# The head of a graph-and-expert kernel: order and engines of the first row tile's loads, statistics and projection

## The chip, the cores and the metric

The kernel runs on one core of a Trainium2 chip. The time is the device time of one execution in microseconds (us), given as the median over several executions. A core has five engines with queues of their own, which wait for each other by semaphores: TensorE (PE; its weight loads are listed as PEld), VectorE (DVE), ScalarE (ACT), GpSimd (POOL) and SyncE (SP), which here issues DMAs only. Sixteen DMA engines move the data of all queues. PE writes its results to PSUM, in banks of 512 float32 per partition; DVE and ACT move them to SBUF.

## The reference

One layer on x (625 rows, 1024 columns) and a graph of 20000 edges with sources `src`, targets `dst` and types 0 or 1. First a graph block, then a mixture of experts; each adds its output to x:

```python
edge_index = jnp.stack([src, dst])
x = x + gnn(layernorm(x), edge_index, edge_type_2, ...)
x = x + ffn(layernorm(x)[None], ...)[0]

def gnn(h, ...):
    n = t5_layer_norm(h, ln_weight)                  # weight * n / rms(n)
    out = n @ W_root + bias                          # 1024 -> 286
    for r in range(2):
        w = (edge_type == r)
        sums = segment_sum((n[src] @ W_rel[r]) * w[:, None], dst)
        out = out + sums / maximum(segment_sum(w, dst), 1)[:, None]
    return h + elu(out) @ wo_weight                  # 286 -> 1024
```

The edges come sorted by target. `ffn` has two shared experts and the best two of eight for each row, with hidden size 256.

## The kernel before, in words

The kernel doesn't gather rows for edges. It counts for each pair (source row, target row and type) how many edges there are, and multiplies that matrix CT by the projected rows. The 625 rows are five tiles of 125 (`TP`, `NT`). The change is in the head of `sparse_kernel`; all behind the counts is left as it is.

*Loads* (lines 520 to 552). Edge types, targets and sources come as 80 rows of 250 numbers, on SP's and ACT's queues. Then x's tile 0, W_root, x's other tiles and the two W_rel on SP's queue, in that order.

*Edge columns* (`edge_columns`, line 664). DVE makes two row arrays `rowf` (source; target key, L667 to L672). PE transposes them into one PSUM bank `p_edge` (L677). ACT copies the keys to float16 columns `cols` (L687), each value twice; DVE splits each source into tile number and place in the tile (L690 to L692), ACT copies the place (L693), and DVE writes a code of the tile number (L695).

*Statistics and h* (`stats`, line 753). For a row tile, DVE runs bn_stats on two halves of x (L757) and bn_aggr (L758), and makes the negative mean `neg` (L760); ACT subtracts the mean from all 1024 columns (`h`, L765). `scales` (line 771) makes the factors from the variance; they are needed only when a projection is moved out of PSUM.

*Columns of h* (`to_columns`, line 789). PE transposes h in eight blocks into two banks (L795); ACT moves the first four (L801) and DVE the other four (L798) to `nT`, scaled by the norm's weight `lT`, which comes from a small transpose (L738, L739).

*Projections* (`project`, line 886). 15 products of a row tile with W_root or one W_rel (L891), 16 matmuls in float32 each. Numbers 0 to 4 are W_root, 5 to 9 and 10 to 14 the two W_rel.

*Counts* (`count_windows`, line 828). The edges are 160 groups of 125 (`EC`). For 4 or 8 of them at a time, DVE makes one-hot matrices of sources (L849, times the code L850) and of keys (L852), and PE multiplies them, a few narrow matmuls for each group (L868), into PSUM. After each group c, `between(c)` issues what was put there by hand with `at(c, ...)` (lines 984 to 1021): statistics, columns, scales, projections, `add_h`, aggregates. Projection 0 stands after group 7, 1 after 15, and 5 to 11 after 46 to 148.

*The order.* A scheduler turns the program into one queue for each engine, mostly in the program's order, by its own estimate of when operands are ready. `tc.issue_after(ins)` puts what is issued in its block behind `ins` on the same engine. PE's `warm(n)` (line 970) issues n matmuls on constants into `scrap` (L972) which nothing reads: 24 ahead of the edge columns and 40 behind them. `ps_mm` and `ps_acc` (lines 494 to 498) are two sets of three PSUM banks.

Of the kernel before, what the change touches and what calls it, by code (L numbers as in the profile page):

```python
# [8 lines left out]
F32 = mybir.dt.float32  # L9
# [9 lines left out]
D = 1024  # L19
# [433 lines left out]
def sparse_kernel(  # L453
# [43 lines left out]
    def ps_mm(name):  # L497
        return psum[0].tile([128, 512], F32, tag="mm", name=name, bufs=3)
# [23 lines left out]
    for name, v, eng in (("ety", edge_type, nc.sync), ("dst", dst, nc.scalar), ("src", src, nc.sync)):  # L522
        ti = fbig.tile([EH, 2 * EP], I32, name=f"{name}_i")
        eng.dma_start(ti, v.rearrange("(c p) -> c p", p=2 * EP))
        rows_i[name] = ti
# [12 lines left out]
    def load_x(t, n):  # L538
        nc.sync.dma_start(xh[:, t : t + n, :], bass.AP(tensor=x.tensor, offset=x.offset + t * TP * D,
                                                       ap=[[D, 128], [TP * D, n], [1, D]]))  # L540

    def load_w(r, w):
        nc.sync.dma_start(wg[:, :, r, :], w.rearrange("(k p) f -> p k f", p=128))

    load_x(0, 1)
    load_w(R, W_root)
# [117 lines left out]
    def edge_columns():  # L664
# [7 lines left out]
        nc.vector.tensor_copy(rowf[:, 0], rows_i["src"])  # L672
        p = ps_mm("p_edge")
        pv = p[:EP, : 2 * EC].rearrange("p (a j c) -> p a j c", a=2, j=2)
        for a in (0, 1):
            for j in range(2):
                nc.tensor.transpose(pv[:, a, j, :], rowf[:, a, j * EP : (j + 1) * EP], ident[:EH, :EH])  # L677
        wide = [EP, EH, 2, 2]

        def column(v):  # L680
            return v.rearrange("p (c j) b -> p c j b", j=2)

        def pairs(v):
            return v.rearrange("p j c -> p c j")[:, :, :, None].to_broadcast(wide)

        with tc.issue_after(table.ins):
            nc.scalar.copy(column(cols[:, KW_]), pairs(pv[:, 1]))  # L687

        q = fbig.tile([EP, 3, 2, EH], F32, name="q")
        nc.vector.tensor_scalar(q[:, 0], pv[:, 0], -float(TP // 2), 1.0 / TP, op0=ALU.add, op1=ALU.mult)  # L690
        nc.vector.tensor_scalar(q[:, 1], q[:, 0], ROUND, -ROUND, op0=ALU.add, op1=ALU.add)
        nc.vector.scalar_tensor_tensor(q[:, 2], q[:, 1], -float(TP), pv[:, 0], op0=ALU.mult, op1=ALU.add)  # L692
        nc.scalar.copy(column(cols[:, SP_]), pairs(q[:, 2]))  # L693

        return nc.vector.tensor_scalar(column(cols[:, VV_].bitcast(I16)), pairs(q[:, 1]), 4096.0, 7168.0,  # L695
                                       op0=ALU.mult, op1=ALU.add)

# [55 lines left out]
    def stats(t):  # L753
        st = small.tile([TP, 2, 6], F32, tag="st", name=f"st_{t}")
        for s in range(2):
            with tc.issue_after((second[0] if t > 1 else evicted[1] if t else behind).ins):
                nc.vector.bn_stats(st[:, s, :], xh[:TP, t, s * 512 : (s + 1) * 512])  # L757
# [3 lines left out]
        h = rows.tile([TP, D], F32, tag="h", name=f"h_{t}")  # L761
        with ExitStack() as order:
            if t == 1:
                order.enter_context(tc.issue_after(evicted[0].ins))
            moved = nc.scalar.activation(h, xh[:TP, t, :], AF.Identity, bias=neg)  # L765
# [61 lines left out]

    def count_windows(between):
        accs = []
        c0 = 0  # L830
        for g in GROUPS:
            oh_s = oneh.tile([EP, MAXG, 128], F16, tag="oh_s", name=f"ohs_{c0}")
            oh_k = oneh.tile([EP, MAXG, KR], F16, tag="oh_k", name=f"ohk_{c0}")

            def both(what, n):
                return [EP, g, n // 2, 2], cols[:, what, c0 : c0 + g][:, :, None, :].to_broadcast([EP, g, n // 2, 2])

            def halves(v):
                return v.rearrange("p g (a b) -> p g a b", b=2)

            order = ExitStack()
            if c0 == 0:
                order.enter_context(tc.issue_after(ahead.ins))
            elif c0 == 8:
                order.enter_context(tc.issue_after(second[0].ins))
            row = iota[:EP].rearrange("p (a b) -> p a b", b=2)
            shape, key = both(SP_, 128)
            os = halves(oh_s[:, :g, :])
            nc.vector.tensor_tensor(os, row[:, None].to_broadcast(shape), key, op=ALU.is_equal)  # L849
            nc.vector.tensor_tensor(os, os, both(VV_, 128)[1], op=ALU.mult)  # L850
            shape, key = both(KW_, KR)
            nc.vector.tensor_tensor(halves(oh_k[:, :g, :]), row[:, None, :SPAN].to_broadcast(shape), key,  # L852
                                    op=ALU.is_equal)
            order.close()
# [120 lines left out]
    warm(24)  # L975
    behind = edge_columns()
    transpose_lnw()
    warm(40)
    ahead = stats(0)
# [7 lines left out]
    for t, (c0, c1) in enumerate(((0, 3), (4, 9), (13, 19), (16, 22), (20, 26))):  # L987
        if t:
            at(c0, stats, t)
        at(c1, to_columns, t, None, nT, True)  # L990
# [11 lines left out]
    at(6, scales, 0, 2)  # L1002
    at(18, scales, 2, 4)
    at(21, scales, 4, NT)
    for i, c in enumerate((7, 15, 21, 24, 28, 46, 64, 82, 100, 118, 134, 148)):
        at(c, project, i)
# [21 lines left out]

    count_windows(between)
# [493 lines left out]
```

## Time and profile before

| what | value |
|---|---|
| median of four runs | 305.6 us (304.04 to 306.76) |
| the profiled execution | 304.4 us, its span 302.2 us |
| mean granted TensorE clock | 0.998 |
| busiest engines | PE 291.3 us, PEld 195.3, DVE 168.3, ACT 107.5 |
| costliest group | L891, 240 matmuls, 62.6 us |
| HBM read and written | 42.76 and 18.81 MB |

The page counts an engine as busy while an instruction of it runs; matmuls are pipelined, so that a busy PE is not PE at its peak. The span starts with the first instruction that the profiler records, and all times of lines count from there. The page's rows of digits cut the span in 40 slices of 7.55 us and give the busy share in tenths. The chain of work is followed back from the last instruction, at each step to what released it. In a timeline row stand start, duration, engine, line, operation, output and inputs, and in brackets how long the engine had been idle and what ended that.

### The profile page before, as it was taken

To read this page: it belongs to the slowest core of one execution; us is meant where nothing else is said; L and a number is where in the kernel's file an instruction comes from. 1 tells how busy PE (TensorE), PEld (TensorE's weight loads), DVE (VectorE), ACT (ScalarE), POOL (GpSimd) and SP (SyncE) were. 2 spreads that over 40 slices of the span, in tenths; PEclk is the share of its full clock that TensorE was granted. 3 is DMA by queue.
4 is the path that set the end of the run, shared out by engine and by line. 5 is a ranking of instruction groups with operands and counts; after the bars stand their busy time and mean duration, and the time that the engine had idled before them with its cause. 6 is when DMAs were issued, how large, how long until landed. Compare 5 with 4: busy or idle time off the path is not lost.

```text
span 302.2 us, 4682 instructions
## 1 busy us (share of the span) xinstructions
PE 291.3 (96%) x1649; PEld 195.3 (65%) x1649; DVE 168.3 (56%) x465; ACT 107.5 (36%) x246; POOL 45.0 (15%) x98
## 2 busy tenths in 40 slices
PE   8899999999999799999999999999999999999992
PEld 6677777787889534476777887887843334444451
DVE  5899999998327568756983122222223212256911
ACT  2455117355334432155123354738269311000000
POOL 9500000000000024240131212210003222200000
PEclk9999999999999999999999999999999999999999
DMA  7999920000009999965999253340056555489352
GB/s 220 318 307 389 421 84 2 0 2 1 0 14 344 348 348 391 399 196 169 353 399 410 86 197 102 109 141 2 0 213 257 221 215 219 176 316 377 138 149 62
DMA packets 27407, 61.15 MB, mean 202 GB/s; under 512 B 2175, under 2 KB 16006, under 8 KB 27374
## 3 DMA queue, kind: packets, MB, share of 16 engines
q1 hardware_dynamic: 21806, 43.77, 40.9%
q0 software_dynamic: 5280, 16.69, 15.9%
q10 hardware_dynamic: 294, 0.35, 0.5%
q8 instruction: 15, 0.25, 0.3%
q14 instruction: 12, 0.10, 0.1%
HBM read 42.76 MB, written 18.81 MB: 204 GB/s over the span
## 4 chain that ended last, share of the span: by engine, by line
PE 93%; DVE 4%; ACT 1%; issue 0%; ACTq 0%
PE p_pr L891 20%; PE p_h L1359 13%; PE p_yj L1417 13%; PE p_o L1472 11%; PE p_sh L1137 10%; PE p_y L952 6%; PE p_agg L909 6%; PE p_x L1340 3%; PE p_t L795 3%; PE cnt L868 2%; PE p_y L956 2%; PE p_hT L1371 1%; PE scrap L972 1%; PE p_gate L1085 1%; PE p_o L1474 1%; DVE ln_4s L727 0%
## 5 line engine op out<-in xcount | busy, mean ns | idle before, releaser
L891 PE MATMUL p_pr<-wg,nT 128*125 128x286 f32 x240 | 62.6, 410 | 0.0
L891 PEld LDWEIGHTS p_pr<-wg,nT 128*125 128x125 f32 x240 | 43.2, 187 | 11.5 <-ACT nT L801 0.5
L1359 PE MATMUL p_h<-w1a,xsT 128*128 (+2 forms) x176 | 40.0, 380 | 0.0
L1417 PE MATMUL p_yj<-w2a,hjT 128*128 (+2 forms) x88 | 38.6, 594 | 0.0
L1472 PE MATMUL p_o<-sw,shT 128*125 128x512 f32 (+1 forms) x88 | 36.1, 553 | 0.0
L1137 PE MATMUL p_sh<-h2T,sw 128*128 128x313 f32 (+1 forms) x128 | 35.2, 428 | 0.0
L1359 PEld LDWEIGHTS p_h<-w1a,xsT 128*128 128x128 f32 (+2 forms) x176 | 28.7, 168 | 7.4 <-issue 0.5
L1137 PEld LDWEIGHTS p_sh<-h2T,sw 128*128 128x128 f32 x128 | 23.7, 189 | 8.6 <-issue 0.2
L1417 PEld LDWEIGHTS p_yj<-w2a,hjT 128*128 128x128 f32 (+2 forms) x88 | 14.4, 168 | 22.4 <-issue 22.4
L1472 PEld LDWEIGHTS p_o<-sw,shT 128*125 128x125 f32 x88 | 16.4, 187 | 16.9 <-issue 16.2
L1421 DVE COPY ys<-p_yj 128x512 f32<-128x512 f32 x15 | 10.4, 692 | 28.7 <-PE p_yj L1417 27.0
L1363 DVE COPY hj<-p_h 128x256 f32<-128x256 f32 x11 | 4.7, 425 | 30.8 <-PE p_h L1359 30.8
L909 PE MATMUL p_agg<-P,CT 125*125 125x287 bf16 x150 | 20.1, 287 | 1.6 <-DVE agg L915 1.6
L909 PEld LDWEIGHTS <-CT 125*125 125x125 bf16 x150 | 18.5, 136 | 2.5 <-issue 2.0
L966 POOL DMA_DIRECT2D x1d<-xh x10 | 5.3, 530 | 98.0 <-DVE xh L959 98.0
L1425 POOL DMA_INDIRECT yt<-ys,row x11 | 10.8, 981 | 50.5 <-DVE ys L1421 50.5
L952 PE MATMUL p_y<-wo_t,eT 128*125 128x512 f32 x40 | 18.1, 595 | 0.0
L1332 POOL DMA_INDIRECT xs<-h2d,tok x11 | 11.1, 1013 | 45.0 <-PE p_x L1340 30.9
L1374 ACT ACTIVATE hjT<-p_hT,vT 128x128 f32<-128x128 f32 (+2 forms) x34 | 8.7, 332 | 24.5 <-PE p_hT L1371 24.5
L1344 DVE COPY xsT<-p_x 128x512 f32<-128x512 f32 x11 | 7.6, 692 | 17.4 <-PE p_x L1340 13.8
L1448 DVE SCALAR_TENSOR_TENSOR x<-p_o,x 125x512 f32<-125x512 f32 (+1 forms) x11 | 6.9, 640 | 16.3 <-PE p_o L1474 16.3
L1359 PE MATMUL p_h<-w1m,xsT 128*64 128x256 f32 (+1 forms) x96 | 14.7, 381 | 0.0
(302 smaller groups left out, 424.4 us busy)
## 6 DMA issues: line engine op xcount, KB each, us to landing
w1a<-in_L_ffn_W_dram SPq DMA_DIRECT2D x8, 1024.0 KB, 10.5
w2a<-in_L_ffn_W_dram SPq DMA_DIRECT2D x8, 1024.0 KB, 5.0
yt<-zero SPq DMA_DIRECT2D x2, 2560.0 KB
g<-yt SPq DMA_DIRECT2D x10, 512.0 KB, 6.6
sw<-in_L_ffn_sW_dram SPq DMA_DIRECT2D x4, 1024.0 KB, 5.0
x<-x1d SPq DMA_DIRECT2D x5, 500.0 KB
wg<-in_L_gnn_W_rel_dram SPq DMA_DIRECT2D x2, 1144.0 KB, 19.8
x1d<-xh POOLq DMA_DIRECT2D x5, 448.0 KB, 6.7
```

Of the source, the lines that this page charges most:

```text
L795: nc.tensor.transpose(pv[:, k, :], row[:, at : at + 128], ident[:TP, :TP])
L891: nc.tensor.matmul(p[:TP, :F], nT[:, k, m * TP : (m + 1) * TP], wg[:, k, r, :], start=(k == 0), stop=(k == KD - 1))
L909: nc.tensor.matmul(p[:TP, : F + 1], CT[:, m, at : at + TP], P[:, m, r, i], start=(m == 0 and i == 0), stop=(m == NT - 1 and i == 2))
L952: nc.tensor.matmul(ps[s][:TP, :], eT[:, k, :], wo_t[:, k, s * 512 : (s + 1) * 512], start=(k == 0), stop=False)
L1137: nc.tensor.matmul(p[:, : z - a], sw1[:, i, k, t * 128 : (t + 1) * 128], h2T[:, k, a:z], start=(k == 0), stop=(k == KD - 1))
L1332: nc.gpsimd.indirect_dma_start(out=xs, out_offset=None, in_=h2d, in_offset=bass.IndirectOffsetOnAxis(ap=tok[:, j : j + 1], axis=0))
L1340: nc.tensor.transpose(p[:, k * 128 : (k + 1) * 128], xs[:, at : at + 128], ident)
L1359: nc.tensor.matmul(p[a:b, :H], xsT[j][:, k, a:b], w1m[j, a][:, 0, k, :] if a else w1a[:, bass.ds(e, 1), k, :], start=(k == 0), stop=(k == ...
L1417: made = nc.tensor.matmul(p[a:b], hjT[:, j, k, a:b], w2m[j, a, k][:, at] if a else w2a[:, bass.ds(e, 1), k, at], start=(k == 0), stop=(k = ...
L1421: nc.vector.tensor_copy(y[:, at], p)
L1425: sent.append(nc.gpsimd.indirect_dma_start(out=yt, out_offset=bass.IndirectOffsetOnAxis(ap=row[:, j : j + 1], axis=0), in_=y, in_offset=No ...
L1472: nc.tensor.matmul(p[:TP, :n], shT[:, i, k, own], sw2[:, i, k, at], start=(i == 0 and k == 0), stop=False)
```

## The change

- The three edge-row loads are all issued on ACT's queue. x's tile 0 becomes the first load on SP's queue, in two halves of 512 columns; W_root follows in two halves of its eight row blocks.
- `edge_columns` ends with the key copy. Its transposes go to two banks, sources to one of `ps_acc`, keys to one of `ps_mm`. The rest is a function of its own, `source_columns`, on DVE alone, which writes the places to `cols` directly; ACT's copy of them and one part of `q` are gone.
- Statistics of tile 0 are put behind the copy of the source rows (L672), ahead of the source columns.
- For tiles 0 and 1, ACT makes the first half of h and DVE the second. The others stay on ACT.
- The columns of tile 0 (`to_columns`) follow in the program ahead of all one-hots, and `one_hots`, taken out of `count_windows`, is called for the first group before that loop; then come statistics of tile 1, the scales of tiles 0 and 1 and projection 0, all ahead of the first count. The first one-hots are put behind the eviction of tile 0's columns, statistics 1 behind the second of these one-hot steps.
- `warm` issues 18 and 14 instead of 24 and 40.
- The hand-placed points move: columns 1 to 4 from 9, 19, 22, 26 to 3, 11, 14, 18; projections 1 to 4 from 15, 21, 24, 28 to 3, 12, 15, 20; 5 to 11 from 46 to 148 to 38 to 146.

```diff
-    for name, v, eng in (("ety", edge_type, nc.sync), ("dst", dst, nc.scalar), ("src", src, nc.sync)):
+    for name, v in (("ety", edge_type), ("dst", dst), ("src", src)):
...
-        eng.dma_start(ti, v.rearrange("(c p) -> c p", p=2 * EP))
+        nc.scalar.dma_start(ti, v.rearrange("(c p) -> c p", p=2 * EP))
...
-    load_x(0, 1)
-    load_w(R, W_root)
+    HALVES = [slice(s * 512, (s + 1) * 512) for s in range(2)]
+    for s in HALVES:
+        nc.sync.dma_start(xh[:, 0, s], x[:128, s])
+    load_w(R, W_root, slice(0, KD // 2), slice(KD // 2, KD))
...
-        nc.vector.tensor_copy(rowf[:, 0], rows_i["src"])
-        p = ps_mm("p_edge")
-        pv = p[:EP, : 2 * EC].rearrange("p (a j c) -> p a j c", a=2, j=2)
+        got = nc.vector.tensor_copy(rowf[:, 0], rows_i["src"])
+        ps = [ps_acc("p_edge"), ps_mm("p_edge_k")]
         for a in (0, 1):
             for j in range(2):
-                nc.tensor.transpose(pv[:, a, j, :], rowf[:, a, j * EP : (j + 1) * EP], ident[:EH, :EH])
...
+                nc.tensor.transpose(ps[a][:EP, j:EC:2], rowf[:, a, j * EP : (j + 1) * EP], ident[:EH, :EH])
 
         with tc.issue_after(table.ins):
-            nc.scalar.copy(column(cols[:, KW_]), pairs(pv[:, 1]))
-
-        q = fbig.tile([EP, 3, 2, EH], F32, name="q")
-        nc.vector.tensor_scalar(q[:, 0], pv[:, 0], -float(TP // 2), 1.0 / TP, op0=ALU.add, op1=ALU.mult)
+            nc.scalar.copy(cols[:, KW_], pairs(ps[1][:EP, :EC]))
+        return got, ps[0][:EP, :EC]
+
+    def pairs(v):
+        return v[:, :, None].to_broadcast([EP, EC, 2])
+
+    def source_columns(v, behind):
+
+        q = fbig.tile([EP, 2, EC], F32, name="q")
+        with tc.issue_after(behind.ins):
+            nc.vector.tensor_scalar(q[:, 0], v, -float(TP // 2), 1.0 / TP, op0=ALU.add, op1=ALU.mult)
         nc.vector.tensor_scalar(q[:, 1], q[:, 0], ROUND, -ROUND, op0=ALU.add, op1=ALU.add)
-        nc.vector.scalar_tensor_tensor(q[:, 2], q[:, 1], -float(TP), pv[:, 0], op0=ALU.mult, op1=ALU.add)
-        nc.scalar.copy(column(cols[:, SP_]), pairs(q[:, 2]))
-
-        return nc.vector.tensor_scalar(column(cols[:, VV_].bitcast(I16)), pairs(q[:, 1]), 4096.0, 7168.0,
+        nc.vector.scalar_tensor_tensor(cols[:, SP_], pairs(q[:, 1]), -float(TP), pairs(v),
                                        op0=ALU.mult, op1=ALU.add)
+
+        nc.vector.tensor_scalar(cols[:, VV_].bitcast(I16), pairs(q[:, 1]), 4096.0, 7168.0,
+                                op0=ALU.mult, op1=ALU.add)
...
-            with tc.issue_after((second[0] if t > 1 else evicted[1] if t else behind).ins):
+            with tc.issue_after((second[0] if t > 1 else first if t else behind).ins):
...
+        own, rest = (HALVES[0], HALVES[1]) if t < 2 else (slice(0, D), None)
...
-            moved = nc.scalar.activation(h, xh[:TP, t, :], AF.Identity, bias=neg)
+            moved = nc.scalar.activation(h[:, own], xh[:TP, t, own], AF.Identity, bias=neg)
+        if rest:
+            with tc.issue_after(last.ins):
+                last = nc.vector.tensor_scalar(h[:, rest], xh[:TP, t, rest], neg, None, op0=ALU.add)
...
+    def one_hots(c0, g):
...
+            if c0 < 8:
+                order.enter_context(tc.issue_after((second[0] if c0 else evicted[1]).ins))
+            nc.vector.tensor_tensor(os, row[:, None].to_broadcast(shape), key, op=ALU.is_equal)
+        last = nc.vector.tensor_tensor(os, os, both(VV_, 128)[1], op=ALU.mult)
...
+        return oh_s, oh_k, last
...
-    warm(24)
-    behind = edge_columns()
+    warm(18)
+    behind, sources = edge_columns()
     transpose_lnw()
-    warm(40)
-    ahead = stats(0)
+    warm(14)
+    source_columns(sources, stats(0))
+    to_columns(0, hs[0], nT, True)
...
-    for t, (c0, c1) in enumerate(((0, 3), (4, 9), (13, 19), (16, 22), (20, 26))):
+    for t, (c0, c1) in enumerate(((0, 3), (6, 11), (9, 14), (13, 18))):
         if t:
-            at(c0, stats, t)
-        at(c1, to_columns, t, None, nT, True)
+            at(c0, stats, t + 1)
+        at(c1, to_columns, t + 1, None, nT, True)
...
-    at(6, scales, 0, 2)
-    at(18, scales, 2, 4)
-    at(21, scales, 4, NT)
-    for i, c in enumerate((7, 15, 21, 24, 28, 46, 64, 82, 100, 118, 134, 148)):
-        at(c, project, i)
+    at(10, scales, 2, 4)
+    at(14, scales, 4, NT)
+    for i, c in enumerate((3, 12, 15, 20, 38, 56, 74, 92, 110, 128, 146)):
+        at(c, project, i + 1)
...
+    oh_s, oh_k, first = one_hots(0, GROUPS[0])
+    made[0] = oh_s, oh_k
+    stats(1)
+    scales(0, 2)
+    project(0)
     count_windows(between)
```

## The prediction

> **What bounds the kernel now.** I read the page first: busy shares, then the slices.
>
> ```profile
> span 302.2 us, 4682 instructions
> PE 291.3 (96%) x1649; PEld 195.3 (65%) x1649; DVE 168.3 (56%) x465; ACT 107.5 (36%) x246; POOL 45.0 (15%) x98
> PE   8899999999999799999999999999999999999992
> DVE  5899999998327568756983122222223212256911
> ```
>
> TensorE (PE) is busy 96% of the span, in nearly every slice of 7.55 us. So time can come only from PE doing something useless, or something useful at a poor time. DVE is full in the third to ninth slice (15 to 68 us): a second engine with no room there. Next, the chain of work that ended last, from the start:
>
> ```profile
> 2.53 2.67 PE scrap L972 x24
> 5.21 0.88 PE p_edge L677 x4
> ...
> 7.52 0.24 DVE cols L695
> 7.76 1.21 DVE st L757 x2
> ...
> 10.62 1.07 PE p_t L795 x8
> 11.70 0.11 PE cnt L868 x4
> 11.81 4.10 PE p_pr L891 x16
> ```
>
> From 10.62 us on the chain is PE, with two holes far behind (96.2 and 128.5 us), neither touched by the change. Before 10.62 PE does little but scrap, and the chain runs edge rows, edge columns, statistics of row tile 0, h, transposes. Here the change acts. The timeline shows the pieces:
>
> ```profile
> 4.06 0.29 DVE L672 CAST rowf<-src_i 80x250 f32<-80x250 int32 x1
> 6.57 0.32 DVE L690 TENSOR_SCALAR q<-p_edge 125x160 f32<-125x160 f32 x1 [2.21 <-ACT cols L687]
> 7.67 1.28 DVE L757 BATCH_NORM_STATS2 st<-xh 125x6 f32<-125x512 f32 x2
> 9.23 0.15 DVE L760 TENSOR_SCALAR neg<-mv 125x1 f32<-125x1 f32 x1
> 9.42 1.15 ACT L765 ACTIVATE h<-xh,neg 125x1024 f32<-125x1024 f32 x1 [1.40 <-DVE neg L760]
> 10.62 1.07 PE L795 MATMUL p_t<-ident,h 125*128 125x125 f32 x8
> 11.79 2.43 PE L891 MATMUL p_pr<-wg,nT 128*125 128x286 f32 x9
> ```
>
> DVE stands idle for 2.21 us behind the ACT copy out of the shared bank p_edge, then makes columns (6.57 to 7.76), then statistics. x of tile 0 is long there: in the trace's DMA packets its 128 packets of 4096 B run from 2.79 to 5.77 us. Last, the windows of half a microsecond, for PE's pace (second column in brackets: matmuls in the stretch):
>
> ```profile
> 6.50:7.00 0.50, 0.50 (x7) 0.50 (x6) 0.40 (x2) 0.10 (x2) 0.50 (x2) 1.00 1.08 384
> 7.50:8.00 0.50, 0.50 (x13) 0.50 (x11) 0.50 (x3) 0.44 (x1) 0.48 (x2) 1.00 1.99 341
> ```
>
> Equal scrap matmuls go at 0.111 us each at first (24 in 2.67 us) and at about 0.055 from 7.0 us on, though the granted clock reads 1.00 throughout.
>
> **The change part by part.** The sum is made on the profiled execution: 304.4 us, of which the span is 302.2. The four runs have a median of 305.6 (304.04 to 306.76), so that execution lies 1.2 under it; I take the gain off the median.
>
> *Loads.* The three edge-row loads all go on ACT's queue. The issues there take 0.43 (dst) and 0.58 us (lnw), so dst is issued at 1.2 instead of 0.74, src at 1.6 instead of 1.19, and ACT's table load moves from 1.81 to about 2.7, ending near 4.2; ACT's next work comes after p_edge, at 5.5 or later, which hides it. ety's use began at 3.16, 2.42 after issue, and src took 2.3 to land: dst would be there at 3.6, where L670 wants it (3.61), src at 3.9, under L672's 4.06. The halves of x are issued on SP at 0.74 and 1.2 instead of 1.65, so they now move beside the rows. The packets give the price: edge rows moved from 1.75 to 2.99; the first sixteen x packets took 0.72 to 1.34 us each, the others 0.159. Rows last behind all of x: some 1.3 us late; not at all disturbed: 0. I take 0.3, since most row packets (46 ns) are short and start before x's would be done. So the copy L672 ends between 4.35 and 5.6, taken 4.65, and x is whole at 4.4 to 5.0, about when its second half is asked for.
>
> *Statistics of tile 0.* From the first bn_stats to the end of neg: 9.38 - 7.67 = 1.71 us. Started at 4.65: neg at 6.4. Before, it was 9.38.
>
> *h in two halves.* ACT took 1.15 us for 1024 elements and 0.36 for 125 (L801), hence some 0.70 for 512: done at 7.1. DVE's half, by L731 (0.82 for 1024), 0.41: done at 6.85, beside ACT's. Key copy (0.42) and lT copy (0.17) precede on ACT, between about 5.8 and 6.5; they hold h up by 0.1 at most.
>
> *Scrap and edge transposes.* 18 instead of 24: 2.47 + 18 x 0.111 = 4.47, so p_edge starts when rowf is there, 4.6 to 5.0, instead of 4.90. p_edge to the next scrap took 1.3 us (4.90 to 6.20): the 14 start at 5.9 to 6.3. At 0.111 up to 7.0 and 0.055 behind, they end at 7.2 to 7.45; all at 0.111, at 7.45 to 7.85. So scrap and h are ready about together, and the transposes start at **7.3** instead of 10.62: **3.3 us**. Ends: 7.05 (rows undisturbed) and 8.3 (rows late).
>
> *Source columns.* One ACT cast (0.47) and one DVE operation go; a scalar_tensor_tensor with 320 outputs comes, 0.3 to 0.55 (L692, L901). All four (1.4 us) now lie between DVE's half of h (6.85) and the eviction of tile 0 (8.4): hidden by transposes. That the key's copy has its own bank ends the 2.21 us wait; late next is the copy L672, then neg.
>
> *First projection ahead of the counts.* From transposes to projection stays 1.17 us (10.62 to 11.79): it starts at 8.5. W_root's packets ran from 4.89 to 10.82, slowed from 7.3 on beside POOL's queue (4576 B packets of 0.64 us median); x leaves some 1.1 us earlier, so W_root should be in by about 7.5 to 9.7. Its second half is needed at 10.5: hidden; without that cover at most 0.3. The four counts that ran in a PE hole at 10.30 now cost: **-0.1**. Behind transposes 0 and 1 no counts fill the wait for the eviction any more: 0.1 each, **-0.2**.
>
> *PE's pace.* With 32 scrap matmuls less, pace could still be slow when transposes begin. In this record it rises at 7.0, so 0; if it rose only 4.5 us (2.47 to 7.0) after the transposes began, half of that, 2.2. I take **-0.1**, nearer the record, since PE stays busy without a break of note from 2.47 on.
> The Trainium skill, page "TensorE: Matmul & The Clock Gate", Part 1, speaks against fewer warm-up matmuls: the clock is halved until PE has been busy for a window of some 3.4 us, and that window runs free, so the moment varies between runs. The row agrees with a doubling, and shows one moment only. By the page alone (an estimate) the rise would fall anywhere from 5.9 to 9.3 us, and the mean loss would be 0.3 instead of 0.1, the time 0.2 longer.
>
> *x of tile 1.* Its packets end at 11.25 now, and statistics 1 start at 12.55. After: evict 0 ends on DVE at 9.2, two one-hot steps 0.7, so statistics 1 want it at 10.0; it should land 1.1 earlier, 10.15. DVE waits with everything queued behind; transposes 1 are wanted when the projection ends (12.7), h1 is ready at 10.15 + 1.71 + 0.7 = 12.55. Ends 0 and 0.8; taken **-0.1**.
>
> *Rows 2 to 4.* DVE must do, before transposes 2 at about 18.1: two evictions 1.3, three one-hot groups 2.6 (0.86 apiece, by starts 9.30 and 10.16), two statistics 3.4, half of h 0.4, scales 1.3: 9.0 from 9.0 on, plus h on ACT behind statistics 2, so 18.35. Ends 0 and 1.5; **-0.2**. The projections from the sixth on come 8 counts earlier, which gives PE work while DVE is behind; PE is no less full, cost 0 (cover: DVE keeping pace; see rivals).
>
> Sum: 3.3 - 0.1 - 0.2 - 0.1 - 0.1 - 0.2 = **2.6 us**. 304.4 - 2.6 = 301.8 for an execution like the profiled one; median 305.6 - 2.6 = **303.0**.
>
> **The rivals.**
> 1. *Everything fits* (transposes at 7.05, none of the four last losses but the counts): 3.55 - 0.1 = 3.4, 302.2. For: each loss is a near fit. Against: five near fits at once.
> 2. *Rows late behind x*: transposes at 8.3, gain 1.6, 304.0. For: the 1 us first packets of x. Against: rows are short packets on another queue.
> 3. *DVE gives it back at the end of the counts.* DVE gains only its 2.21 + 0.63 idle, less two halves of h (0.8) and the later rows (0.3): 1.7. The last counts start at 73.09, DVE's last one-hots end at 72.3, so PE may gain 1.7 + 0.8 = 2.5 before it waits there; if the last projections do not move ahead and DVE loses a further 1 to x of tile 1: 1.5, 304.1.
> 4. *Slower: DVE sets the pace of the first rounds.* Should one-hot groups of 8 (0.68 + 0.68 + 0.4 = 1.7 us) stand in DVE's queue ahead of statistics 2, 3 and 4, transposes wait. Slack before transposes 4 is 1.6 us (DVE's work 17.6 from 8.5, plus h 1.2, is 27.3; PE gets there at 28.9). It decides at 2.6 + 1.6 = 4.2 us of such work, 2.5 groups. One group for each of three rounds: 5.1 - 4.2, 306.5; two: 10.2 - 4.2, 311.6; middle 309. For: DVE is full from 15 to 68 us. Against: statistics are asked for three to nine counts ahead of their transposes.
>
> **How the numbers follow.** Forecast 0.48 (its own range 302.1 to 303.9: transposes at 7.05 without the small losses but the counts, to 7.85 with 0.4 more of them), rival 1 0.20, rival 2 0.12, rival 3 0.11, rival 4 0.09. About 1% (3.06 us; 302.54 and 308.66) is what a measurement tells from no change. Faster by over 1%: rival 1 and three tenths of the forecast (0.44 of its range's 1.8, and some scatter of medians), 0.20 + 0.14 = 0.34. Slower by over 1%: most of rival 4, 0.07. Within: 0.59. Range: 301.3 (rival 1 less 0.9 of scatter, a third of the 2.7 between the runs before) to 305.2 (rivals 2 and 3 with about as much); outside lie rival 4 and a tenth of the rest.
>
> **What would show it.** Right: p_t first at 7.0 to 7.6, p_pr at 8.2 to 8.8, no DVE idle behind the key's copy, neg at 6.1 to 6.7, scrap pace doubling before 7.5. Wrong: L672 ending after 5.2 (rows late); PE waiting on h or x before transposes 1 or 2 for over 0.8; matmuls of the first projection at half pace; DVE ending its one-hots later than 70.8, with PE waiting there.

## The result

| | before | after | ratio, 95% interval |
|---|---|---|---|
| median | 305.04 us (303.62 to 307.36, 78 runs) | 305.72 us (304.49 to 308.13, 52 runs) | 1.0028 [1.0018, 1.0037] |
| profiled execution, its span | 304.4, 302.2 | 306.45, 304.5 | |

No difference by the 1% bound, and a little slower: 0.7 us, against a forecast of 2.6 less. 305.72 lies 0.5 above the range. The profiled pair stands 2.1 apart, three times what the medians say, so a profile's times show where something was lost and not what it is worth; prices below are by medians, or by the ratio to before on the same chip where that is said.

The page of the kernel after, the same four lines as shown of before:

```profile
span 304.5 us, 4623 instructions
PE 291.6 (96%) x1617; PEld 194.5 (64%) x1617; DVE 169.1 (56%) x467; ACT 106.6 (35%) x245; POOL 45.0 (15%) x98
PE   4999999999999799999999999999999999999992
DVE  4799999999526758765884122212223212238920
```

PE's first slice falls from 8 to 4: scrap is gone, and a hole is there instead. DVE's full stretch now ends a slice later (the tenth digit is 9, it was 8, and the eleventh 5 instead of 3). DVE is busy 0.8 us longer in all.

The chain of waits of after, from the start, and the first piece behind the projections, which will serve as a milestone (60 aggregate matmuls; in before they start at 88.77):

```profile
1.67 5.12 DMA src_i<-in_src_dram
6.88 0.30 DVE rowf L675
7.31 0.68 PE p_edge L679 x2
...
8.61 1.60 PE scrap L983 x14
10.22 1.67 PE p_t L802 x8
11.88 5.06 PE p_pr L902 x16
17.06 0.91 PE p_t L802 x8
...
90.85 7.47 PE p_agg L920 x60
```

The chain begins with a DMA of 5.12 us, which was not in it before. Transposes 0 start 0.4 to 0.6 us earlier than before (10.22 here, 10.01 by the timeline; 10.62 before), transposes 1 some 1.1 later, and by the milestone the kernel is 2.1 behind. The timeline of after:

```profile
4.17 0.42 DVE L670 TENSOR_TENSOR rowf<-ety_i,low 80x250 f32<-80x250 int32 x1 [1.42 <-DMA ety_i<-in_edge_type_dram]
5.67 0.42 DVE L673 SCALAR_TENSOR_TENSOR rowf<-dst_i,rowf 80x250 f32<-80x250 int32 x1 [1.09 <-DMA dst_i<-in_dst_dram]
6.88 0.29 DVE L675 CAST rowf<-src_i 80x250 f32<-80x250 int32 x1 [0.79 <-DMA src_i<-in_src_dram]
8.64 0.15 DVE L762 TENSOR_SCALAR neg<-mv 125x1 f32<-125x1 f32 x1
8.83 0.73 ACT L769 ACTIVATE h<-xh,neg 125x512 f32<-125x512 f32 x1
8.83 0.49 DVE L772 TENSOR_SCALAR h<-xh,neg 125x512 f32<-125x512 f32 x1
10.01 1.87 PE L802 MATMUL p_t<-ident,h 125*128 125x125 f32 x8
11.68 5.27 PE L902 MATMUL p_pr<-wg,nT 128*125 128x286 f32 x16
```

Three brackets in a row say the same: DVE waits for an edge row three times, 3.3 us in all, and the source copy ends at 7.17 where the forecast had 4.65. From there to neg and to h all goes as long as forecast. Then two durations stand out: eight transposes in 1.87 us (1.07 before) and 16 matmuls in 5.27 (4.10). In the trace's DMA packets the 240 row packets, 1.75 to 2.99 us before, now run from 2.32 to 6.15, mixed in time with x's first tile (1.77 to 4.60) and W_root (from 3.97). SP's own waits show one thing more:

```profile
SPq L539 <- DMA ety_i<-in_edge_type_dram: 1.4, 1, 1.4
...
SPq L553 <- DMA dst_i<-in_dst_dram: 0.6, 1, 0.6
SPq L544 <- DMA src_i<-in_src_dram: 0.3, 1, 0.3
```

(Waiting line, what was waited for, us in total, times, longest.) SP, which only issues loads, now waits for the edge rows to land; x of tile 1 is issued at 4.08 instead of 2.59. In after statistics 1 lose nothing by it: they start at 13.57 without a wait for x.

### The profile page after: what moved, and what is told of

The parts are those of the page before. It is cut to its first block, busy times and chain, and to the rows that moved or that the text cites. A ratio compares the mean times of both kernels' runs of the same rounds, so it can differ in the third digit from the quotient of the medians.

```text
span 304.5 us, 4623 instructions
## 1 busy us (share of the span) xinstructions
PE 291.6 (96%) x1617; PEld 194.5 (64%) x1617; DVE 169.1 (56%) x467; ACT 106.6 (35%) x245; POOL 45.0 (15%) x98
## 4 chain that ended last, share of the span: by engine, by line
PE 89%; DVE 6%; DMA 2%; ACT 1%; issue 1%; ACTq 0%; DVEq 0%
PE p_pr L902 17%; PE p_h L1375 13%; PE p_yj L1433 13%; PE p_o L1488 11%; PE p_sh L1153 10%; PE p_y L963 6%; PE p_agg L920 6%; PE p_x L1356 3%; PE p_t L802 2%; PE p_y L967 2%; DMA src_i<-in_src_dram 2%; PE cnt L879 2%; DVE st L759 1%; PE p_hT L1387 1%; PE p_gate L1101 1%; PE p_o L1490 1%
## 5 line engine op out<-in xcount | busy, mean ns | idle before, releaser
L902 PE MATMUL p_pr<-wg,nT 128*125 128x286 f32 x240 | 64.7, 416 | 0.1
```

The costliest lines, as they stand in the source:

```text
L902: nc.tensor.matmul(p[:TP, :F], nT[:, k, m * TP : (m + 1) * TP], wg[:, k, r, :], start=(k == 0), stop=(k == KD - 1))
```

## The experiments

Two theories stood at first. A: the late rows take the gain. B: PE's half pace takes it. Two more came up early. C: DVE, full from some 15 us on, sets the pace of the rounds and when the counts end, so that an earlier start of PE is given back there. D: x of tiles 1 and 2 lands too late for an earlier start. A table first; times in us, the last three columns by each profile (the last one-hot of DVE ends; the last counts of PE start; the milestone).

| run | median | ratio to before | one-hots | counts | milestone |
|---|---|---|---|---|---|
| before | 305.04 | | 72.3 | 72.9 | 88.77 |
| after | 305.72 | 1.0028 [1.0018, 1.0037] | 75.5 | 75.6 | 90.85 |
| e1 rows first | 307.02 | 1.0060 [1.0033, 1.0086] | 76.6 | 76.7 | 91.94 |
| e2 rows on one queue | 307.53 | 1.0081 [1.0050, 1.0112] | 78.0 | 78.1 | 93.32 |
| e3 more scrap | 305.11 | 1.0002 [0.9979, 1.0026] | 74.2 | 74.2 | 89.50 |
| e4 loads alone, on before | 306.30 | 1.0046 [1.0025, 1.0066] | 74.4 | 75.0 | 90.82 |
| e5 e1, bias late | 305.05 | 1.0018 [0.9984, 1.0051] | 74.3 | 74.4 | 89.65 |
| e6 e5, more scrap | 305.78 | 1.0002 [0.9971, 1.0033] | 74.3 | 74.4 | 89.66 |
| e7 bias late, on before | 304.20 | 0.9966 [0.9945, 0.9986] | 72.2 | 72.8 | 88.66 |
| e8 e1, more scrap | 306.81 | 1.0047 [1.0021, 1.0074] | 76.1 | 76.2 | 91.46 |
| e9 after, add_h late | 304.04 | 0.9987 [0.9966, 1.0008] | 63.4 | 73.0 | 88.88 |
| e10 e6, x split | 303.61 | 0.9966 [0.9948, 0.9983] | 73.3 | 73.3 | 88.58 |
| e11 e6, points earlier | 304.17 | 0.9969 [0.9947, 0.9992] | 76.9 | 79.2 | 91.06 |
| e12 all together | 301.78 | 0.9920 [0.9891, 0.9949] | 63.6 | 74.8 | 86.71 |
| e13 before, add_h late | 305.11 | 1.0019 [1.0000, 1.0039] | 61.4 | 73.3 | 89.17 |
| e14 before, three helpers | 304.76 | 1.0001 [0.9989, 1.0014] | 60.6 | 72.5 | 88.37 |
| e15 after, h on ACT | 305.05 | 1.0012 [0.9992, 1.0031] | 75.0 | 75.0 | 90.31 |
| e16 after, three helpers | 304.03 | 0.9929 [0.9900, 0.9959] | 64.2 | 73.9 | 89.77 |
| e17 e12, rows late | 303.95 | 0.9940 [0.9906, 0.9973] | 66.1 | 77.3 | 89.17 |
| e18 e12, less scrap | 302.90 | 0.9884 [0.9846, 0.9922] | 65.3 | 76.5 | 88.39 |

The ratio is to before on the same chip. Before's median read 304.7 to 305.1 there, but 306.35 beside e16 to e18 (single runs from 303.4 to 307.3), so that these three ratios flatter: by medians against 304.8, e16 is 0.8 us under before and not 2.2. A profile is one execution; that of e11 (306.14) lies 2 us above its median.

**e1 and e2: the rows.** The rows' loads as in before, ahead of x on two queues; or all on SP, ahead of x.

```diff
-    for name, v in (("ety", edge_type), ("dst", dst), ("src", src)):
-        nc.scalar.dma_start(ti, ...)
+    for name, v, eng in (("ety", edge_type, nc.sync), ("dst", dst, nc.scalar), ("src", src, nc.sync)):
+        eng.dma_start(ti, ...)        # e2: nc.sync for all three
```

> The changed kernel with its edge-row loads put back as they were (types and sources on SP ahead of x, targets on ACT); the order on PE, DVE and ACT is the changed one. Theory A (the rows come 2.8 us late because x's halves and W_root share the DMA engines with them): the copy of the source rows ends at 4.4 to 4.8 instead of 7.16, first transposes at 7.4 to 8.0 instead of 10.0, first projection at full pace; time 302.5 to 304.2. Theory B (the scrap matmuls taken out leave PE at slow pace): the first projection still takes 4.6 us or more, time 304.6 or more. Theory C (DVE sets the pace of the first rounds): the transposes of tile 0 come early, those of tile 2 no earlier than 20.5 (before 20.96), time 304.2 to 305.2.

> The changed kernel with all three edge-row loads on SP's queue ahead of x, so that they are one queue's first three loads but x and W_root come behind them. Theory A: third issue at 1.65, landing 2.3 later, so the source copy ends by 4.5 as in the run with the rows put back, and the time is within 0.5 us of it. Rival (three loads one after the other on one queue are what is slow): the source copy ends at 5.5 or later and the time is within 0.7 us of the changed kernel's 305.7.

e1 lies far above what theory A gave, and by medians both are slower than after (by 1.3 and 1.8). The timeline of e1:

```profile
3.97 0.29 DVE L675 CAST rowf<-src_i 80x250 f32<-80x250 int32 x1
...
8.27 1.93 PE L802 MATMUL p_t<-ident,h 125*128 125x125 f32 x8 [0.96 <-ACT h L769]
9.99 4.98 PE L902 MATMUL p_pr<-wg,nT 128*125 128x286 f32 x16
13.75 1.29 DVE L759 BATCH_NORM_STATS2 st<-xh 125x6 f32<-125x512 f32 x2 [1.79 <-DMA xh<-in_x_dram]
...
16.28 1.08 PE L802 MATMUL p_t<-ident,h 125*128 125x125 f32 x8 [1.20 <-ACT h L769]
```

The rows are mended to the tenth (the copy ends at 4.26, in e2 at 4.08), and transposes 0 start 1.7 us earlier than in after. And yet nothing comes of it: statistics 1 start at 13.75 for want of x (13.57 in after), and transposes 1 at 16.28, still 0.5 behind before (15.80). In e2 statistics 1 wait 2.01, statistics 2 another 2.87. A alone falls as the cause of the time; the late rows are real, but x is next (D). e2 also shows that sharing one queue isn't what makes rows late, since its rows are the earliest: what delays them in after is x, whose packets start first. (Rows on ACT's queue with x held back were not run.)

**e3: the pace.** 24 more scrap matmuls ahead of the edge columns, in PE's hole.

```diff
-    warm(18)
+    warm(42)
```

> The changed kernel with 42 instead of 18 scrap matmuls ahead of the edge columns, which fill PE's 2.7 us hole while it waits for the rows; loads as changed. Theory A: h still comes at 9.6, only the pace is mended (first projection 4.1 instead of 5.1 us, transposes 0.9 instead of 1.7): 304.2 to 305.0. Theory B: the pace was all that was lost: 303.0 to 303.7. If DVE is the limit behind (theory C), nothing comes of it: 305.3 to 305.9.

```profile
9.51 1.07 PE L802 MATMUL p_t<-ident,h 125*128 125x125 f32 x8 [0.61 <-ACT h L769]
14.79 1.07 PE L802 MATMUL p_t<-ident,h 125*128 125x125 f32 x8
20.34 1.07 PE L802 MATMUL p_t<-ident,h 125*128 125x125 f32 x8
```

Pace is full here (1.07, and the projection 4.12): PE's scrap speeds up at 5.9 us. PE runs ahead of before by 1.1 us at transposes 0, 1.0 at transposes 1 and 0.6 at transposes 2 (20.96 in before). By the milestone it is 0.7 behind. B alone is worth 0.6 us by medians and 0.8 by ratios, and not the 1.7 that the profile lost; the rest goes between 20 and 75 us, where DVE is full.

**e4: the loads alone.** The kernel before with the loads of after, nothing else.

> The kernel before with the changed order of loads alone (rows on ACT, x's tile 0 and W_root in halves and first on SP). Theory A: the source copy ends at 7.0 to 7.3 instead of 4.35, and all behind it moves by 2.0 to 2.8 us: 307.0 to 307.9. Theory B: with all 64 scrap matmuls in place the time stays near that before, 305.0 to 305.6. Theory C: DVE is late by as much, so as theory A.

306.3: 1.3 us by medians (ratio 1.0046: 1.4), less than A gave and more than B. The source copy ends at 7.50, statistics 0 start at 9.89 instead of 7.67 and transposes 0 at 12.83 instead of 10.62, with PE at full pace. So the loads cost 2.2 us at that place, of which some three fifths show in the median.

**e5 to e8: x and the bias.** The convolution's bias goes to all 125 partitions in one load on POOL's queue. In e1's packets it moves from 7.4 to 11.2 us, 31 packets of 4576 B, 0.2 to 1.6 us each; beside it a few of W_root's packets take up to 0.45 us, where most take 0.05. e5 is e1 with this load on SP, behind x's last tile; e6 has 24 scrap matmuls instead of 14 as well, e7 is the kernel before with the bias late, e8 is e1 with the 24.

```diff
-    nc.gpsimd.dma_start(cb, bcast_rows(conv_bias, TP))
...
+    nc.sync.dma_start(cb, bcast_rows(conv_bias, TP))     # behind x, ahead of W_rel
...
-    warm(14)
+    warm(24)                                             # e6, e8
```

> The run with the rows put back, and the load of the bias cb taken off POOL's queue and put on SP's behind x's last tile. Theory D (with the rows in time the next limit is the landing of x's tiles 1 and 2 and of W_root's tail, held up by the 31 packets of 4576 B of the bias, 0.6 us each, at 7.4 to 11.2 us): statistics 1 start by 11.7 instead of 13.75, those of tile 2 do not wait for x at 17.75, transposes of tile 2 by 21.5 instead of 22.8; time 304.3 to 305.5 against 307.0, the first projection still at slow pace. Theory C (DVE's work, not x, sets the rounds): no change from 307.0 beyond 0.5.

> The same with 24 instead of 14 scrap matmuls behind the edge transposes, so that PE does not stand idle before tile 0's transposes. If landing and pace together are what ate the gain (D with B): first projection 4.1 us from about 9.4 on, transposes 1 by 14.2, transposes 2 by 20.3; time 302.7 to 304.0, faster than both kernels. If DVE sets the rounds (C): as the run without the added scrap, within 0.4.

> Control: the kernel before with the bias moved in the same way. It never waited for x's tiles 1 to 4 or W_root, so by theory D nothing comes of it: 304.7 to 305.4. A gain of over 0.5 would mean that the bias costs something beyond the head's loads.

> The run with the rows put back with 24 instead of 14 scrap matmuls behind the edge transposes, bias left on POOL's queue: pace alone. Theory D: x's tile 1 still lands at 13 to 14, so a faster first projection only waits longer: 306.2 to 307.2. Theory B (pace): 304.8 to 305.7.

e5 takes 2 us off e1: statistics 1 start at 11.60 without a wait, where e1 waited to 13.75. That is D, and it is the bias. But e5 is no faster than before. (Its statistics 2 still wait 1.28 us for x.) e6 has transposes 1 at 14.43 (before 15.80) and transposes 2 at 20.52 (20.96), and is no faster either, against a forecast of 302.7 to 304.0: its pace isn't mended (the projection takes 4.57), and DVE's last one-hots end at 74.3, 2.0 later than in before. e8, with the wait for x, gives nothing for its better pace: transposes 1 wait 1.33 us for h. e7 was to show nothing and gained 1.0 us by its ratio, with no transposes of its head moved by over 0.1; in e14, which has the same edit and two more, that gain isn't there. I take it for the size of error that such a ratio can have between builds; that `add_h` late hides it in e14 isn't excluded, since that edit alone reads 0.6 slower in before (e13).

**e9 and e13: DVE's load.** The five `add_h` (DVE adds h to x, for the layer's output) stand between the one-hots; they are moved behind the last count, in after and in before.

```diff
-    for t in range(NT):
-        at(40 + 16 * t, add_h, t)
...
+    for t in range(NT):
+        at(EC - 1, add_h, t)
```

> The changed kernel with its five add_h (DVE, 1.28 us each, between counts 40 and 104) moved behind the last count, where DVE has room; nothing else changed. Theory C (DVE, full from 20 us to its last one-hots at 75.5, is what PE's counts wait for): the last one-hots end near 70, the 0.5 us that PE falls back between 50 and 80 us comes back; the 1.7 lost before 30 us stay: 304.9 to 305.4 against 305.7. Rival (PE has work enough of its own there, DVE is only busy): no change, 305.5 to 305.9.

> The kernel before with one edit: the five add_h of each half, which DVE does between the one-hots, moved behind the last count. Theory C (in after DVE's one-hots set the end of the counts, in before they do not, since there the last one-hots end at 72.3 us and the last counts start at 73.09): 0 to 0.3 us, 304.7 to 305.1. Rival (the move is worth the same in any kernel of this kind, by what it takes off DVE and PE's semaphores, and the 1.7 us that it brought in after say nothing about after): 303.4 to 304.2.

The timelines at the end of the counts (DVE's last one-hot, PE's last counts), of before, after, e13 and e9:

```profile
71.65 0.68 DVE L850 TENSOR_TENSOR ohs<-ohs,cols 125x1024 f16<-125x1024 f16 x1
72.92 0.46 PE L868 MATMUL cnt<-ohk,ohs 125*128 125x58 f16 x11
```

```profile
75.13 0.39 DVE L857 TENSOR_TENSOR ohk<-iota,cols 125x464 f16<-125x464 f16 x1
75.58 0.37 PE L879 MATMUL cnt<-ohk,ohs 125*128 125x58 f16 x8
```

```profile
60.70 0.69 DVE L850 TENSOR_TENSOR ohs<-ohs,cols 125x1024 f16<-125x1024 f16 x1
73.32 0.46 PE L868 MATMUL cnt<-ohk,ohs 125*128 125x58 f16 x11
```

```profile
62.94 0.41 DVE L857 TENSOR_TENSOR ohk<-iota,cols 125x464 f16<-125x464 f16 x1
72.98 0.51 PE L879 MATMUL cnt<-ohk,ohs 125*128 125x58 f16 x13
```

In after the last counts start 0.06 us behind the end of the last one-hot, and 0.05 or 0.06 behind in e1, e2, e3, e5, e6, e8, e10 and e15 too, though their counts start anywhere from 73.3 to 78.1; in before 0.59 behind. The five `add_h` are 6.4 us of DVE (1.28 each); without them DVE's last one-hots come 11 us sooner in before and 12 in after, since some of the moves out of PSUM now also stand behind them. In before the counts come no sooner for it (73.32) and the time doesn't fall (305.11). In after the time falls by 1.7 us by medians, more than C gave, and by 1.2 by the two ratios, whose intervals don't overlap.

The counts of e9 come 2.6 earlier than those of after, but not all of that is the edit's. Transposes 1 of after and of e9, which stand ahead of every `add_h`:

```profile
16.90 1.05 PE L802 MATMUL p_t<-ident,h 125*128 125x125 f32 x8
```

```profile
15.67 1.08 PE L802 MATMUL p_t<-ident,h 125*128 125x125 f32 x8
```

1.2 us were there already, in a head that is the same program: e9's rows landed 0.4 earlier, and its PE reached full pace at 12.0 us instead of 14.1. From transposes 1 to the milestone after takes 73.95 us, e9 73.2 and e16 (below, it has the edit too) 73.0; before takes 73.0 and e13 73.4. So the edit is worth 0.7 to 0.9 us of that stretch and 1.2 to 1.7 of the time in after, and nothing in before: C holds, DVE's queue up to the last one-hot became a bound of that stage through the change. In before it is 0.6 us from being it. PE shows no hole for it; it is busy all the time from 70 to 80 us in after as well:

```profile
70.00:80.00 10.00, 10.00 (x63) 7.77 (x62) 8.25 (x17) 8.14 (x23) 0.00 (x0) 1.00 0.01 2
```

Matmuls of the projections behind (two at 74.27, two at 74.97) stand between the last counts there, so that no single wait shows the loss.

**e15: less on DVE, later transposes.** After, with h of tiles 0 and 1 whole on ACT.

```diff
-        own, rest = (HALVES[0], HALVES[1]) if t < 2 else (slice(0, D), None)
+        own, rest = slice(0, D), None
```

> The kernel after with h of row tiles 0 and 1 whole on ACT, so that DVE is relieved of two halves (0.49 us each) and transposes 0 wait some 0.45 us longer for h. Theory C (DVE's work up to the last one-hots sets the end of the counts): the last one-hots end 0.5 to 1 us earlier (75.5 in after) and the time falls by 0.3 to 0.8, to 304.9 to 305.4. Rival (the start of the transposes counts): 0.3 to 0.5 slower, 306.0 to 306.2.

305.05, ratio 1.0012 [0.9992, 1.0031] against 1.0028 of after: by medians 0.7 less, though transposes 0 start later (10.35); the last one-hots end 0.5 earlier (75.0), with the counts right behind. The intervals overlap, and the profile of e15 also has the faster projection (4.12 instead of 5.27), which the edit doesn't touch, so it leans to C and doesn't show it alone.

**e10 to e12: a version that uses the start.** e10 is e6 with x of tiles 2 and 3 in separate loads; e11 is e6 with the hand-placed points (scales too) earlier and projection 12 ahead of the last count; e12 has all of it and `add_h` late.

```diff
-    load_x(2, 2)
+    load_x(2, 1)
+    load_x(3, 1)                                                            # e10, e12
...
-    for t, (c0, c1) in enumerate(((0, 3), (6, 11), (9, 14), (13, 18))):
+    for t, (c0, c1) in enumerate(((0, 3), (3, 5), (5, 7), (7, 9))):           # e11, e12
...
-    for i, c in enumerate((3, 12, 15, 20, 38, 56, 74, 92, 110, 128, 146)):
+    for i, c in enumerate((3, 6, 8, 10, 28, 46, 64, 82, 100, 118, 136, 150)):
```

> The run with rows put back, bias late and more scrap, with x's tiles 2 and 3 in a load each instead of one of 1 MB. There statistics 2 waited for x until 15.49 and the transposes of tile 2 for h. Theory D (landing of x): statistics 2 start by 14.2, transposes 2 at 19.7 instead of 20.5, time 0.4 to 0.9 below that run (304.8 to 305.4). Theory C: DVE is behind by its own work, under 0.3 comes of it.

> The same run (rows put back, bias late, more scrap) with hand-placed points moved: columns 2, 3, 4 behind counts 5, 7, 9 instead of 11, 14, 18, projections 2 to 4 behind 6, 8, 10, the others 10 counts earlier, number 12 inside the counts. DVE has then 6 to 10 one-hot groups of work less to do ahead of the transposes, and PE more work ahead of each count. Theory C: the lead of 1.3 us that PE had at 15 us is kept, 303.3 to 304.6. Theory D (x of tiles 2 to 4 lands too late for earlier rounds): DVE waits for x and the time is 305.2 to 306.

> All of these together: rows put back, bias late, more scrap, x's tiles 2 and 3 apart, points moved, add_h late. If C and D with the slow pace are all that eats the gain, it beats both kernels and the one before with the bias late (304.2): 302.5 to 303.8. If something else behind the head takes it (the end of the counts, aggregates), 304.2 or more.

e10 and e11 are about 1 us under before, e12 is 3.0 under it by medians and 2.4 by its ratio, faster than both kernels. In e10 statistics 2 start at 14.40 with no wait for x, in e6 at 15.49 behind a wait of 1.13. e10 leaves DVE's work as it is in after, and yet it is 2.1 us under after: of the two, loads and pace on one side and DVE on the other, neither is the whole of the loss. The chain of waits of e12:

```profile
8.49 1.56 PE p_t L803 x8
14.24 1.07 PE p_t L803 x8
15.34 4.12 PE p_pr L903 x16
19.52 0.89 PE p_t L803 x8
...
86.71 7.47 PE p_agg L921 x60
```

Transposes 0, 1 and 2 are 2.1, 1.7 and 1.6 us ahead of before, and the milestone 2.1: now the early start lasts, with the last one-hots done at 63.6. The earlier points of e11 and e12 were not tried in before, so how much of e12's lead over before the change itself earns isn't shown.

**e14 and e16: whose gain is it?** The three helpers (bias late, x split, `add_h` late) in the kernel before and in the kernel after, with nothing else.

> The kernel before, nothing of the change, with the helpers of the best version: bias loaded late on SP, x of tiles 2 and 3 in separate loads, add_h late. The best version (the change, its edge rows first, more scrap, points moved, and the same helpers) took 301.8. Theory C with D (the change's earlier start is worth 2 us once DVE and the loads are mended): 303.6 to 304.3 here. Rival (all that was gained is the helpers', and the change's order gives nothing even then): 301.5 to 302.6.

> The kernel after with the three helpers of which the kernel before gained nothing (304.76 against 304.74): bias late on SP, x of tiles 2 and 3 in separate loads, add_h behind the last count. Edge rows and scrap stay as in after. With DVE's bound gone, theory says the change's order pays here: 302.0 to 303.5, the rest up to the best version (301.8) being the late rows, the slow pace and the points. Rival (late rows and pace take all of it once DVE is no bound): 304.0 to 304.8.

In before they are worth nothing (1.0001 [0.9989, 1.0014]), less than either side forecast. In after they make 305.72 into 304.03, 1.7 us. So what they gain depends on the change. That the change with them then beats before isn't shown: e16 lies in the range of its rival (late rows and slow pace take all of it), 0.8 us under before by medians of different chips, and e7 has read 1.0 for an edit that moved no transposes. Its milestone (89.77) is 1.1 ahead of after's and 1.0 behind before's.

**e17 and e18: late rows and pace in the best version.** e12 with the rows behind x as in after; e12 with `warm(14)`.

> The best version (301.8) with one thing put back: the three edge-row loads on ACT's queue behind x's first half, as in after. In after their delay was 2.8 us and mending it alone gave nothing. If the delay counts once DVE and the loads are mended (theory A under C): 302.8 to 304.0. Rival (it is covered there too): 301.5 to 302.3.

> The best version (301.8) with the 14 scrap matmuls of after behind the edge columns instead of 24. Theory B under C (PE's slow pace through transposes 0 and projection 0 costs what it takes, some 1.5 us in the profiles, once nothing else waits): 302.3 to 303.3. Rival (the ten scrap matmuls only take the place of slow useful ones): 301.5 to 302.1.

By the profiles each costs what was first supposed: with late rows transposes 0 start at 11.12 instead of 8.28 and the milestone is 2.5 later; with less scrap the first projection crawls:

```profile
9.97 6.03 PE L903 MATMUL p_pr<-wg,nT 128*125 128x286 f32 x16
```

(4.09 in e12), and the milestone is 1.7 later. By medians they stand 2.2 and 1.1 above e12. But that is between two chips, and the ratios of the three overlap, so these two prices are likely and not shown. What is seen is that with x and DVE out of the way the head's losses reach the milestone; the better pace of e8 brought it only 0.5 us there against e1.

## Why the prediction failed, step by step

Three terms failed, and they hang together. The 3.3 us of earlier transposes were 0.6, since the rows came 2.5 us late (*Loads*). The 0.1 for PE's pace was 1.65 in the profile, since with 32 scrap matmuls less and a hole ahead of the edge transposes PE stayed at half pace until 14.1 us (*PE's pace*). And the cover of *Rows 2 to 4*, DVE keeping pace, was priced at 0; taking 6.4 us of other work off DVE there brings 1.2 to 1.7 us. Transposes 2, forecast for 18.35, start at 22.17 (in before at 20.96), so that by the profile most of the loss was made ahead of them.

- *Loads*: failed first. The copy was to end at 4.65, at the latest at 5.6; it ended at 7.17. The bound from above took the worst to be rows that come last behind all of x, 1.3 us. They came last behind x and beside W_root, and with x's packets in front, 240 packets that had needed 1.24 us needed 3.83. This is rival 2, worse than its bound: transposes at 10.01, where it had 8.3. The Trainium skill, page "DMA: Bandwidth & Descriptors", section "Queues, rings and completion order", says that each DMA engine goes round its queues packet by packet; the packets of the two queues do run mixed in time here, and 2.6 us were lost all the same. SP's wait for the rows wasn't in the prediction at all. The price alone is 1.3 us (e4).
- *Statistics of tile 0*: right, 1.71 us from bn_stats to the end of neg (7.08 to 8.79), only started late.
- *h in two halves*: right in length (0.73 and 0.49, forecast 0.70 and 0.41). On DVE the two tiles are 0.98 us, 0.8 in rival 3 and only partly in the sum; they lie in DVE's queue ahead of the one-hots.
- *Scrap and edge transposes*: 14 matmuls in 1.60 us, at the slow end of what was given; the transposes gained 0.6 instead of 3.3. The copy of the rows was 2.5 late, and scrap and h were not ready together: h was done at 9.56, and the transposes stood behind scrap until 10.01.
- *Source columns*: right, no one waits for them.
- *First projection ahead of counts*: W_root was there in time, as said (in e2 the projection waited 0.81 for it). The gap from transposes to projection was 1.67 instead of 1.17, which is pace.
- *PE's pace*: mis-sized. 0.1 was taken, 2.2 given as the end, for a rise 4.5 us behind the first transpose; it came 4.1 behind. From the first transpose to the end of the projection after took 6.94 us and before 5.29: 1.65 in the profile, 0.6 to 0.8 by e3. The reason given, "PE stays busy without a break of note", was wrong, since the late rows leave it idle for 2.75 us ahead of the edge transposes; e3, which fills that hole with scrap, has full pace from 5.9 us. The rows alone don't explain it: with rows in time and the same scrap (e1) full pace still came at 11.9, with ten scrap matmuls more and no hole (e6) at 10.9.
- *x of tile 1*: forecast 10.15, with an end of 0.8. In e1, where the rows were early, x came at 13.75: 3.6 late. In after itself nothing waited for it. The bias's packets were seen (they stand in the prediction as POOL's queue) and weighed for W_root only.
- *Rows 2 to 4* and its "cost 0 (cover: DVE keeping pace)": this failed too (e9 against e13). It was rival 3's place, and its sign was right ("DVE ending its one-hots later than 70.8"), its size not: rival 3 had DVE 1.7 us ahead, where it came 3.2 behind. The windows from 3 to 20 us, of before and of after, say how (behind the stretch and its length: busy us and, in brackets, instructions of PE, PEld, DVE, ACT, POOL, then granted clock, DMA share, GB/s):

```profile
3.00:20.00 17.00, 15.69 (x127) 13.51 (x126) 13.57 (x44) 7.12 (x18) 8.82 (x28) 1.00 1.01 304
```

```profile
3.00:20.00 17.00, 14.22 (x78) 11.69 (x77) 11.70 (x36) 5.59 (x15) 8.76 (x28) 1.00 1.05 315
```

  DVE works 11.70 us there instead of 13.57: 1.87 us more idle, first for the rows, then for the slow transposes (from 10.6 to 12.0, since the first one-hots are put behind the eviction of tile 0's columns). With the 0.98 for halves of h and about 0.17 for the longer place operation that is 3.0 us, and its last one-hots come 3.2 later. An engine with no room from 15 to 72 us can't win back what it loses before 15.

Of the four signs of being wrong two came as written, L672 ending after 5.2 and the first projection at half pace, and a third in part: one-hots later than 70.8, with no wait of PE to be seen. The likeliest class, within 1%, came true by luck: it was given for a gain of 2.6 us, and the number was 2.7 off.

## What to carry to other kernels

Where two engines are both full behind the place of a change, an earlier start is worth only as much as the second one's queue moves too: count that engine's idle and added time ahead of the stage as carefully as the first one's chain. A test for it is cheap: take work off that engine in the kernel before and in the kernel after, and see in which one the time answers. And a load that is put ahead of another is a change of that other load: bound it by what was in front, not by how short it is. Where losses stand one behind the other, mending the first alone may show nothing, or less than nothing (e1); that doesn't clear it.

## What the runs showed of the hardware beyond what was expected

- Small loads beside the start of a big one on another queue: 240 packets of 1000 B took 1.24 us from first to last when they were issued ahead of x, and 3.83 when x's 256 packets of 2048 B were issued at the same times on the other queue. On one queue ahead of x they took 1.47, and the copy was done earliest (4.08).
- A load spread to 125 partitions on POOL's queue had 31 packets of 4576 B of 0.2 to 1.6 us in e1. Moved behind x it let statistics 1 start at 11.60 with no wait for x, instead of 13.75 (e5 against e1).
- PE's pace doubles in the first 16 us of each of these runs, at a moment that moves by several us (in e4 it fell back once, at 8.6, before it rose for good at 12.0). In the windows of after (the first number in brackets is the matmuls in half a microsecond)

```profile
9.00:9.50 0.50, 0.50 (x8) 0.50 (x6) 0.50 (x2) 0.50 (x1) 0.00 (x0) 1.00 0.74 275
...
12.50:13.00 0.50, 0.50 (x2) 0.36 (x2) 0.50 (x2) 0.00 (x0) 0.50 (x1) 1.00 1.05 426
...
14.50:15.00 0.50, 0.50 (x4) 0.39 (x3) 0.47 (x2) 0.00 (x0) 0.01 (x1) 1.00 1.03 215
```

  scrap goes at the slow pace (8 here; in before 7 at the slow and 13 at the full pace), so does the projection at first (2), and then it goes at full pace (4), all with a granted clock of 1.00. By the spacing of equal matmuls (scrap 0.107 or 0.056 us, projection 0.48 or 0.24) full pace begins at 7.1 us in before, 5.9 in e3, 9.0 in e8, 9.9 in e12, 10.9 in e6, 12.0 in e9, 14.1 in after and 14.0 in e16; after, e9 and e16 have the same head. The Trainium skill, page "TensorE: Matmul & The Clock Gate", Part 1, has the clock at half until PE has been busy for a window of some 3.4 us, which runs free, and halved again after an idle window of that length. Counted from the first scrap (2.47) that is an estimate of 5.9 to 9.3 us, and before and e3 lie in it; after, with its hole of 2.75 us, lies in it when counted from the scrap behind the hole (8.55), at 12.0 to 15.4. e6 has no hole in PE's record and lies outside it when counted from 2.47; counted from its second scrap (5.70), 9.1 to 12.5, it lies inside. What of the work in between counts as busy isn't shown here.
